# A second split in five products for two of layer 0's aggregates, with their left sums made one item per opportunity

## The chip, the cores and the metric

The kernel runs on one core of one Trainium2 chip. The metric is device time of one execution in microseconds (us), lower is better; where several executions were timed, the median is used. One execution was also taken by the hardware profiler, and all durations of single stages come from it.

## The reference

Two layers of a graph network on N = 2708 nodes with D = 1024 features, all fp32, `adj` an N×N matrix of 0 and 1:

```
# layer 0
h = relu(layernorm(x))
f = h @ Wf + bf;  g = h @ Wg + bg
e = relu(f @ g.T)                      # N x N
a = softmax(where(adj > 0, e, -9e15), axis=1)
x = x + a @ (h @ W + bW)
# layer 1
h = relu(layernorm(x)) @ W1
e = leaky_relu(h @ a1 + (h @ a2).T, 0.2)
a = softmax(where(adj > 0, e, -9e15), axis=1)
x = x + relu(a @ h)
```

The large parts are products of matrices: scores (N×D by D×N), the aggregate of the attention with the rows of h (N×N by N×D), and the projections (N×D by D×D). In layer 0 the kernel computes the aggregate of h first and multiplies it by W afterwards.

## The kernel before

**Tiling.** The N nodes for which attention is computed are split in NP = 5 panels of 576, 576, 532, 512 and 512 columns. Everything is kept transposed: an attention tile S holds 128 source nodes on its partitions and one panel's columns. The source nodes form NQ = 10 pairs of 128-row tiles and two left-over tiles (MONO and TINY); two pairs form a group, and there are NK = 5 groups. W = 512 is half of D, WH = 256 a quarter.

**Products.** Each big product is a 2×2 Strassen–Winograd product: seven products named M1, M5, M2, M6, M3, M7, M4 of half-size operands in place of eight. Their left operands are sums of rows of h, made once and kept in DRAM: `hg_d` for layer 0, `hr_d` for layer 1. Their right operands are sums of halves of attention tiles. A panel's halves are 288, 288, 266, 256 and 256 columns wide.

**Stages.** For each panel of layer 0 the program runs: scores (line 1425), then the left side of the next panel's scores (`project_q`), then the aggregate (`aggregate`, whose matmuls are at line 679 in `accumulate`), then the projection by W (`project`, line 1314). Panel 3's projection comes after panel 4's scores. Layer 1 has an aggregate and a projection per panel.

**The aggregate of layer 0.** `accumulate` runs one product after another. A product is 80 matmuls: 10 pairs × 2 tiles' halves, 4 column blocks `d`. The left operand is loaded by SP (line 139) as 512 KB tiles `hc`, one per product and group. Sums collect in PSUM banks gx (M1, M2), gy (M5, M3), gz (M6, M7), gv (M4), and gw for the left-over rows (`into_m15`, line 971). VectorE (its additions are all recorded at line 45) or ScalarE empties the banks; the results of each node column are multiplied by 1/sum at the end, in GpSimd for three of four blocks (`scale`, line 1021).

**The aggregate of layer 1.** Panels 1 to 4 of layer 1 use another function, `aggregate_quartered` (from line 1087). There every one of the seven products is split once more in seven: 20 matmuls of a quarter of the panel's columns each (`product`, line 1114), on banks gx, gy, gz and gu. The right sums ("quarter" tiles) come from `make`, 20 VectorE operations per product. The left sums are four more blocks in DRAM, `hs2_d`. They are prepared by work items that `put_quarters` creates, one per product and group: GpSimd reads the rows (`hq`, line 417), VectorE does four operations of 128x256, and GpSimd stores two blocks (line 143).

**Order of the work.** Work items stand in lists (`lazy`, `later`) and are run in program order at opportunities, the calls of `behind(rate)`: four per product of `accumulate` (after k = 2, 5 and 7 and at the product's end). Each call gives credit of `rate` (3.0 in layer 0), and an item costs what `put` was given, 1.7 for an item of `put_quarters`. `ahead[0]` items have their reads issued ahead of the one that runs. Each engine keeps the program's order; a tile framework assigns buffers and sets waits. The pools concerned are 54 `slot` buffers, 12 `stream` buffers of 4 KB per partition, and 8 PSUM banks.

The call around the change is in the main loop over panels:

```
spare[0], from_slots[0] = p > 0, p == NP - 1
G[p] = aggregate(0, p, S, got["sm"], then)
```

Of the kernel before, what the change touches and what calls it, by code (L numbers as in the profile page):

```python
# [57 lines left out]
def kernel(  # L58
# [95 lines left out]
    groups = [[q, q + 1] for q in range(0, NQ, 2)]  # L154
    group_of = {q: (i, j) for i, g in enumerate(groups) for j, q in enumerate(g)}
    assert sorted(group_of) == list(range(NQ))
    hg_d = [dram.tile([P, 7, len(g), W], FP, name=f"hg_d{i}") for i, g in enumerate(groups)]
    NK = NQ // 2
    WH = W // 2
    hr_d = dram.tile([P, 7, 2, 2, NK, WH], FP, name="hr_d")  # L160
    hs2_d = dram.tile([P, 7, 4, NK, WH], FP, name="hs2_d")
# [206 lines left out]
    def rows_h(q, ha, hb):  # L368

        i, j = group_of[q]  # L370
        for m, h in ((M1, ha[0]), (M5, ha[1]), (M2, hb[0]), (M4, hb[1])):
            store(hg_d[i][:, m, j], h)
# [3 lines left out]
    def sums_h():  # L376

        def fetch(q, two):
            i, j = group_of[q]
            for m in (M1, M2):  # L380
                two.append(stream("hr", (P, 2, W)))
                (load if "m" in got else by_scalar)(two[-1], hg_d[i][:, m:m + 2, j])
# [6 lines left out]
        def second(q, two):  # L389
# [3 lines left out]
            i, j = group_of[q]  # L393
            store(hg_d[i][:, M6:M7 + 1, j], two[0])
            store(hg_d[i][:, M3, j], b0)
            store(hg_d[i][:, M5, j], b1)
# [6 lines left out]
    BY_QUARTERS = (M1, M5, M2, M6, M7, M3, M4)  # L403
    made_quarters = {}

    def put_quarters(m, k, to=lazy):
# [3 lines left out]
        def fetch():  # L410
            if from_slots[0]:
# [7 lines left out]
        def go():  # L419
# [5 lines left out]
            for h in range(2):  # L425
                store(hs2_d[:, m, 2 * h:2 * h + 2, k], two[h])
            made_quarters[m] = made_quarters.get(m, 0) + 1
        put(1.7, go, fetch, to=to)

    def quarters_until(m):  # L430
        while made_quarters.get(m, 0) < NK:
            one(lazy if lazy else later)
# [491 lines left out]
    def aggregate(l, p, S, sm, then={}, rate=3.0):  # L924
# [29 lines left out]
        steps = [(m, i) for m in order_of_products for i in range(len(groups))]  # L954

        def left(m, q, d):
            i, j = group_of[q]
            at = steps.index((m, i))
            for m_, i_ in steps[at:at + (3 if l else 1)]:
                if (m_, i_) not in hc:  # L960
                    hc[m_, i_] = stream("hc", (P, 4, WH) if l else (P, 2, W))
                    load(hc[m_, i_], hr_d[:, m_, :, :, i_].rearrange("p h f c -> p (h f) c") if l else hg_d[i_][:, m_])
# [71 lines left out]
    def quarters_of(p, S):  # L1034
# [50 lines left out]
        return {"make": make, "right": right, "first": first, "fifth": fifth, "second": second, "fourth": fourth}  # L1085

    def aggregate_quartered(p, S, sm, of_right, then={}, fine=1.2):
# [12 lines left out]
        def product(m, n, ps, start):  # L1100
            quarters_until(m)
            if (m, 0) not in lasts:
                for i, of in enumerate((hr_d[:, m, :, :, NK - 1].rearrange("p h f c -> p (h f) c"), hs2_d[:, m, :, NK - 1])):
                    lasts[m, i] = stream("hl2", (P, 4, WH))
                    load(lasts[m, i], of)
# [3 lines left out]
            load(t, hr_d[:, m, i // 2, i % 2, :NK - 1] if raw else hs2_d[:, m, i, :NK - 1])  # L1109
# [11 lines left out]
        def left_over(banks, e, s, fresh):  # L1121

            two = stream("hl", (P, W + 2 * P))
            load(two, hgl_d[1][:, e])
# [44 lines left out]
        def with_second():  # L1169
# [4 lines left out]
                       M7: lambda: make(M3), M3: lambda: make(M4)}  # L1174
        left_out = None
        for m in BY_QUARTERS:
            V = [quad(*direct[m])[:, 2 * r:2 * r + 2] for r in range(2)] if m in direct else [v[:, :, :h] for v in in_pairs("V")]
# [40 lines left out]
            if m == M5:  # L1218
                of_right["second"]()
            if m == M5:  # L1220
                inverse.append(inverse_sums(p, sm))
# [357 lines left out]
    def rows_done(t, xt):  # L1579
# [14 lines left out]
        if panel_of[t] == NP - 1:  # L1594
# [18 lines left out]
            else:  # L1613
# [16 lines left out]
                if q == NQ - 1:  # L1630
                    for m in BY_QUARTERS:
                        put_quarters(m, q // 2, later)
# [17 lines left out]
        elif whole:  # L1650
# [3 lines left out]
            if quads_met[q // 2] == 2:  # L1654
                put(0.0, lambda: [put_quarters(m, q // 2) for m in BY_QUARTERS])
# [12 lines left out]
    ORDERED = (NP - 1,)  # L1668

# [98 lines left out]
    for p in range(NP):  # L1768
# [21 lines left out]
        G[p] = aggregate(0, p, S, got["sm"], then)  # L1790
        spare[0] = False
        if p == 0:
            flush()
# [156 lines left out]
```

## Time and profile before

| what | value |
|---|---|
| median of 3 runs | 3051.23 us (3044.36 to 3053.49) |
| profiled execution | 3049.19 us, of which the profiler's span is 3047.3 |
| TensorE (PE) busy | 2993.9 us, 98% of the span |
| VectorE (DVE) busy | 2047.6 us, 67% |
| ScalarE (ACT), GpSimd (POOL) busy | 536.8 us, 496.9 us |
| TensorE clock granted | 0.997 of full speed |
| DMA | 766.78 MB, mean 252 GB/s |
| layer 0's aggregates of panels 1, 2, 3 | 148.2, 137.1 and 132.0 us |

PE is the matmul part of TensorE and PEld its weight loads, which overlap it. SP issues the loads, and its queue is that of line 139. A share of busy time is an average over all stages; a stage is read from a window of its own. Buffer numbers are left out of tile names, so `hs_d` also stands for `hs2_d`.

### The profile page before, as it was taken

The numbers are of one execution on the slowest core, as the hardware profiler recorded it, in microseconds if no ns is written. First come the engines' busy times: TensorE is split into PE (matmuls) and PEld (weight loads), VectorE is DVE, ScalarE is ACT, GpSimd is POOL, SyncE is SP. The second block draws the span as 40 slices with busy tenths as digits, with TensorE's granted clock in tenths as the row PEclk, the third lists the DMA queues.
The fourth block names the chain that finished last, engine by engine and source line by source line (L and its number), as shares of the span: only waits on it lengthen the run. The fifth ranks groups of instructions, "written<-read, shape, count | busy, mean of one in ns | idle before, by whom it ended". The sixth has DMA issues, their size and how long they took to land.

```text
span 3047.3 us, 41722 instructions
## 1 busy us (share of the span) xinstructions
PE 2993.9 (98%) x14642; PEld 2294.2 (75%) x14642; DVE 2047.6 (67%) x4667; ACT 536.8 (18%) x880; POOL 496.9 (16%) x770
## 2 busy tenths in 40 slices
PE   8998999999999999999999999999999999999999
PEld 4576777667877588885888886784767959879695
DVE  5776794585742686616965276867878768887863
ACT  4420020020200121101210111302232121212200
POOL 1421111210112110223111111131212010020201
PEclk9999999999999999999999999999999999999999
DMA  6989878887466786768957588679768768878887
GB/s 232 302 271 272 311 276 308 264 286 235 133 236 165 228 273 195 247 156 251 292 188 251 179 241 258 223 292 335 245 212 264 263 202 299 294 265 297 264 294 268
DMA packets 392704, 766.78 MB, mean 252 GB/s; under 512 B 65728, under 2 KB 206944, under 8 KB 392464
## 3 DMA queue, kind: packets, MB, share of 16 engines
q1 hardware_dynamic: 332336, 584.80, 59.6%
q0 software_dynamic: 54464, 164.78, 16.1%
q10 hardware_dynamic: 5696, 14.55, 1.4%
q8 instruction: 116, 1.90, 0.2%
q14 instruction: 92, 0.75, 0.1%
HBM read 630.04 MB, written 138.11 MB: 252 GB/s over the span
## 4 chain that ended last, share of the span: by engine, by line
PE 73%; DVE 11%; issue 8%; DMA 5%; POOL 1%; ACT 1%; SPq 1%; POOLq 0%; DVEq 0%; ACTq 0%
PE sz L1425 6%; PE gy L679 6%; PE gz L679 6%; PE gz L1114 5%; PE gx L679 5%; PE sx L1425 4%; PE pz L1314 4%; PE sy L1425 4%; PE px L1314 4%; PE py L1314 3%; PE gy L1114 3%; PE gx L1114 3%; PE gv L679 3%; PE M_ps L591 3%; PE qz L679 2%
## 5 line engine op out<-in xcount | busy, mean ns | idle before, releaser
L1425 PE MATMUL sz<-B,As 128*128 128x288 f32 (+2 forms) x1200 | 292.0, 392 | 6.0 <-DVE st L45 5.1
L1425 PEld LDWEIGHTS sz<-B,As 128*128 128x128 f32 x1200 | 227.2, 190 | 55.2 <-DVE st L45 8.4
L1425 PE MATMUL sx<-B,As 128*128 128x288 f32 (+2 forms) x800 | 200.8, 394 | 12.4 <-DMA As<-hs_d 10.4
L1425 PE MATMUL sy<-B,As 128*128 128x288 f32 (+2 forms) x800 | 199.0, 392 | 0.0
L1425 PEld LDWEIGHTS sx<-B,As 128*128 128x128 f32 x800 | 152.5, 191 | 45.8 <-DMA As<-hs_d 9.5
L679 PE MATMUL gz<-Sa,hc 128*128 128x288 f32 (+2 forms) x800 | 185.8, 392 | 0.0
L679 PEld LDWEIGHTS gz<-Sa,hc 128*128 128x128 f32 x800 | 151.5, 190 | 32.2 <-issue 2.2
L1425 PEld LDWEIGHTS sy<-B,As 128*128 128x128 f32 x800 | 151.7, 190 | 30.6 <-DVE st L45 0.3
L1114 PE MATMUL gz<-quarter,hc 128*128 128x128 f32 (+2 forms) x1344 | 168.8, 279 | 3.8 <-DVE gT L45 3.7
L1114 PEld LDWEIGHTS gz<-quarter,hc 128*128 128x128 f32 x1344 | 160.6, 191 | 5.1 <-DVE gT L45 4.6
L143 POOL DMA_DIRECT2D out_dram<-x_res x164 | 81.2, 502 | 469.1 <-DVE x_res L45 461.9
L1314 PE MATMUL py<-w,ps 128*128 128x512 f32 x320 | 142.0, 593 | 0.0
L1314 PE MATMUL pz<-w,ps 128*128 128x512 f32 x320 | 142.0, 594 | 0.0
L1314 PE MATMUL px<-w,gT 128*128 128x512 f32 x320 | 141.1, 593 | 0.0
L679 PE MATMUL gy<-T,hc 128*128 128x288 f32 (+2 forms) x480 | 114.9, 402 | 3.8 <-DMA hc<-hg_d 3.8
L1314 PEld LDWEIGHTS pz<-w,ps 128*128 128x128 f32 x320 | 60.2, 190 | 76.2 <-issue 72.2
L1314 PEld LDWEIGHTS py<-w,ps 128*128 128x128 f32 x320 | 60.5, 190 | 75.1 <-issue 72.7
L591 PE MATMUL M_ps<-wgT,wfT 128*128 128x512 f32 x256 | 112.7, 596 | 1.6 <-ACT hsT L45 1.6
L1314 PEld LDWEIGHTS px<-w,gT 128*128 128x128 f32 x320 | 60.1, 190 | 71.3 <-issue 67.8
L679 PEld LDWEIGHTS gy<-T,hc 128*128 128x128 f32 x480 | 93.1, 194 | 24.7 <-DMA hc<-hg_d 4.3
L143 POOL DMA_DIRECT2D mk_d<-mask x55 | 35.9, 654 | 456.4 <-DVE mask L45 439.4
L45 ACT ACTIVATE P<-P 128x576 f32<-128x576 f32 (+3 forms) x111 | 72.1, 650 | 207.3 <-DVE P L45 207.2
(391 smaller groups left out, 5819.6 us busy)
## 6 DMA issues: line engine op xcount, KB each, us to landing
hc<-hg_d SPq DMA_DIRECT2D x175, 512.0 KB
As<-hs_d SPq DMA_DIRECT2D x150, 512.0 KB
hc<-hr_d SPq DMA_DIRECT2D x119, 512.0 KB
hc<-hs_d SPq DMA_DIRECT2D x112, 512.0 KB
w<-wt_d SPq DMA_DIRECT2D x96, 512.0 KB
w<-in_L_gnn_W_dram SPq DMA_DIRECT2D x72, 512.0 KB
md<-md_d SPq DMA_DIRECT2D x56, 512.0 KB
adj_i<-in_adj_dram SPq DMA_DIRECT2D x200, 128.0 KB
```

The source lines that it names most:

```text
L45: i = f(*a, **k)
L143: nc.gpsimd.dma_start(a, b)
L591: nc.tensor.matmul(ps, wfT[a][c // NH][:, c % NH, :], wgT[b][c], start=(c == 0), stop=(c == NC - 1))
L679: nc.tensor.matmul(ps[d], left(m, k, d), right(m, k), start=(start and k == 0), stop=(k == K - 1), skip_group_check=True)
L1114: nc.tensor.matmul(ps[:, d], lhs[:, d * P:(d + 1) * P], inner_right(m, n, k), start=(start and k == 0 and d == 0), stop=(k == NK - 1), ski ...
L1314: nc.tensor.matmul(ps, left[i][m][:, k, :], w_[k], start=(start and k == 0), stop=(k == NH - 1), skip_group_check=True)
L1425: nc.tensor.matmul(ps[:n, :h], lefts[q][:, i % 2, c, :n], B[m][c // 2][:, c % 2, :h], start=(start and c == 0), stop=(c == NH - 1), skip_g ...
```

## The change

- `hg_d` was five tiles, one per group; it becomes one tile, indexed by group and pair.
- `hs2_d` becomes a pair, one tile per layer.
- `SPLIT_EARLY = (2, 3)`: in layer 0 the aggregates of panels 2 and 3 use `aggregate_quartered`, at a rate of 3.0 with 1.2 after each quarter product. In it, layer 0 keeps M1 and M5 as plain products through `accumulate`; M2, M6, M7, M3 and M4 are split in seven each. M1's banks are emptied by eight ScalarE copies, M5's by four VectorE additions; the products' 2×2 blocks V are collected in two `stream` tiles each; the factor 1/sum is applied by VectorE.
- `make(M2)`, the right sums of the first split product, is called in the middle of M5, and the sums of columns after it.
- `put_quarters` gets the layer as an argument. For layer 0 an item reads one 512 KB block of `hg_d` and has a cost of 3.0, one item per opportunity. The 25 items (five products, five groups) are put when panel 0's aggregate ends, ahead of the items of layer 1 that are left from before, so they run in panel 1's aggregate.

The diff, cut to its core:

```diff
-    hg_d = [dram.tile([P, 7, len(g), W], FP, name=f"hg_d{i}") for i, g in enumerate(groups)]
+    hg_d = dram.tile([P, 7, NK, 2, W], FP, name="hg_d")
-    hs2_d = dram.tile([P, 7, 4, NK, WH], FP, name="hs2_d")
+    hs2_d = [dram.tile([P, 7, 4, NK, WH], FP, name=f"hs2_d{l}") for l in range(2)]
...
-    BY_QUARTERS = (M1, M5, M2, M6, M7, M3, M4)
+    BY_QUARTERS = ((M2, M6, M7, M3, M4), (M1, M5, M2, M6, M7, M3, M4))
     made_quarters = {}
 
-    def put_quarters(m, k, to=lazy):
+    def put_quarters(l, m, k, to=lazy):
 
         two = []
 
         def fetch():
+            if l == 0:
+                t = stream("hq", (P, 2, 2, WH))
+                nc.gpsimd.dma_start(t.rearrange("p f h c -> p f (h c)"), hg_d[:, m, k])
+                two.extend(t[:, :, h] for h in range(2))
+                return
             if from_slots[0]:
                 two.extend(slot(f"hq{h}", (P, 2, WH)) for h in range(2))
             else:
...
             sub(a11, a22, a11)
             sub(a12, a12, a11)
             for h in range(2):
-                store(hs2_d[:, m, 2 * h:2 * h + 2, k], two[h])
-            made_quarters[m] = made_quarters.get(m, 0) + 1
-        put(1.7, go, fetch, to=to)
-
-    def quarters_until(m):
-        while made_quarters.get(m, 0) < NK:
+                store(hs2_d[l][:, m, 2 * h:2 * h + 2, k], two[h])
+            made_quarters[l, m] = made_quarters.get((l, m), 0) + 1
+        put(1.7 if l else 3.0, go, fetch, to=to)
+
+    def quarters_until(l, m):
+        while made_quarters.get((l, m), 0) < NK:
             one(lazy if lazy else later)
     u = consts.tile([P, NC], FP, name="u")
...
         def fourth():
             for q in range(NQ):
                 sub(t1(q), wb_(q)[:, lo], wa_(q)[:, lo])
-        return {"make": make, "right": right, "first": first, "fifth": fifth, "second": second, "fourth": fourth}
-
-    def aggregate_quartered(p, S, sm, of_right, then={}, fine=1.2):
+        return {"make": make, "right": right, "operand": operand, "first": first, "fifth": fifth, "second": second, "fourth": fourth}
+
+    def aggregate_quartered(l, p, S, sm, of_right, then={}, fine=1.2, rate=3.0):
...
         lasts = {}
         def product(m, n, ps, start):
-            quarters_until(m)
+            quarters_until(l, m)
             if (m, 0) not in lasts:
-                for i, of in enumerate((hr_d[:, m, :, :, NK - 1].rearrange("p h f c -> p (h f) c"), hs2_d[:, m, :, NK - 1])):
+                rows = hr_d[:, m, :, :, NK - 1] if l else hg_d[:, m, NK - 1].rearrange("p f (h c) -> p h f c", h=2)
+                for i, of in enumerate((rows, hs2_d[l][:, m, :, NK - 1])):
                     lasts[m, i] = stream("hl2", (P, 4, WH))
-                    load(lasts[m, i], of)
+                    if l or i:
+                        load(lasts[m, i], of if i else of.rearrange("p h f c -> p (h f) c"))
+                    else:
+                        for h_ in range(2):
+                            load(lasts[m, i][:, 2 * h_:2 * h_ + 2], of[:, h_])
             t = stream("hc2", (P, NK - 1, WH))
             raw = n in (M1, M2, M4)
             i = {M1: 0, M2: 1, M4: 3, M6: 0, M3: 1, M7: 2, M5: 3}[n]
-            load(t, hr_d[:, m, i // 2, i % 2, :NK - 1] if raw else hs2_d[:, m, i, :NK - 1])
+            load(t, hs2_d[l][:, m, i, :NK - 1] if not raw else hr_d[:, m, i // 2, i % 2, :NK - 1] if l else
+                 hg_d[:, m, :NK - 1, i % 2, i // 2 * WH:(i // 2 + 1) * WH])
             last = lasts[m, int(not raw)][:, i]
             for k in range(NK):
                 for d in range(2):
...
         def left_over(banks, e, s, fresh):
             two = stream("hl", (P, W + 2 * P))
-            load(two, hgl_d[1][:, e])
+            load(two, hgl_d[l][:, e])
             cols = lambda b: slice(s.start + b * hb, s.start + (b + 1) * hb)
             for (a, b), ps in banks.items():
                 for d in range(2):
...
         before_next = {M1: lambda: make(M5), M5: with_second, M2: lambda: (of_right["fourth"](), make(M6)), M6: lambda: make(M7),
                        M7: lambda: make(M3), M3: lambda: make(M4)}
+        def sums_of_columns():
+            of_right["second"]()
+            inverse.append(inverse_sums(p, sm))
+
+        def collected():
+            if l == 0:
+                return [stream("V", (P, 2, h)) for r in range(2)]
+            return [v[:, :, :h] for v in in_pairs("V")]
+
+        if l == 0:
+            hc = {}
+
+            def left(m, q, d):
+                i, j = q // 2, q % 2
+                if (m, i) not in hc:
+                    hc[m, i] = stream("hc", (P, 2, W))
+                    load(hc[m, i], hg_d[:, m, i])
+                return hc[m, i][:, j, d * P:(d + 1) * P]
+
+            def first_product(d, ps):
+                nc.scalar.copy(quad(0, lo)[:, d], ps)
+                nc.scalar.copy(quad(1, lo)[:, d], ps)
+            exps_until(NQ)
+            of_right["fifth"]()
+            accumulate(left, of_right["operand"], NQ, h, (M1, M5), then,
+                       {M1: first_product, M5: lambda d, ps: add(quad(0, hi)[:, d], ps, quad(0, lo)[:, d])}, "g",
+                       {M5: sums_of_columns}, rate=rate, by_k=True, more={(M5, NQ // 2): with_second})
+
         left_out = None
-        for m in BY_QUARTERS:
-            V = [quad(*direct[m])[:, 2 * r:2 * r + 2] for r in range(2)] if m in direct else [v[:, :, :h] for v in in_pairs("V")]
+        for m in BY_QUARTERS[l]:
+            V = [quad(*direct[m])[:, 2 * r:2 * r + 2] for r in range(2)] if m in direct else collected()
             c11, c12 = (V[0][:, :, b * hb:(b + 1) * hb] for b in range(2))
             c21, c22 = (V[1][:, :, b * hb:(b + 1) * hb] for b in range(2))
             X = bank2("gx")
...
                 into_place(m, V, 1)
                 scale(m, 1)
             if m == M5:
-                of_right["second"]()
-            if m == M5:
-                inverse.append(inverse_sums(p, sm))
+                sums_of_columns()
             if m in then:
                 then[m]()
         left_out()
...
         return list(full(p)) + ([MONO, TINY][p - 1:p] if p in (1, 2) else [])
     ORDERED = (NP - 1,)
+    SPLIT_EARLY = (2, 3)
     def by_gpsimd(o, i, **k):
         tc.keep_in_program_order(nc.gpsimd.dma_start(o, i, **k))
...
             then[M6] = lambda: first_masks(NP - 1, 1)
             then[M7] = lambda: first_masks(NP - 1, 2)
         spare[0], from_slots[0] = p > 0, p == NP - 1
-        G[p] = aggregate(0, p, S, got["sm"], then)
+        if p in SPLIT_EARLY:
+            G[p] = aggregate_quartered(0, p, S, got["sm"], quarters_of(p, S), then)
+        else:
+            G[p] = aggregate(0, p, S, got["sm"], then)
         spare[0] = False
         if p == 0:
+            for m in BY_QUARTERS[0]:
+                for k in range(NK):
+                    put_quarters(0, m, k)
             flush()
             ahead[0] = 2
             for s in range(1, NP):
...
             then = dict(zip((M2, M6) if p else (M3, (M7, "middle")), (lambda p=p: take_shifts(p + 1), lambda p=p: take_weights(p + 1))))
         spare[0] = p < 2
         ahead[0] = 2 if p else 4
-        g = aggregate_quartered(p, S, sm, next_right, then, fine=1.0) if p else aggregate(1, p, S, sm, then, rate=4.0)
+        g = aggregate_quartered(1, p, S, sm, next_right, then, fine=1.0) if p else aggregate(1, p, S, sm, then, rate=4.0)
         hooks = {}
         if p + 1 < NP:
             next_right = quarters_of(p + 1, got["P"][0])
```

## The prediction

> **What bounds the kernel now.** I read the page's engine totals and slices first, then the chain of waits, then a table of windows over the stages that the diff touches.
>
> ```profile
> PE 2993.9 (98%) x14642; PEld 2294.2 (75%) x14642; DVE 2047.6 (67%) x4667; ACT 536.8 (18%) x880; POOL 496.9 (16%) x770
> PE   8998999999999999999999999999999999999999
> PEclk9999999999999999999999999999999999999999
> ```
>
> TensorE works 98% of the span at full clock. The share is an average, so the windows decide. Their columns are the window, its length, each engine's busy time, clock, DMA share and GB/s; the rows are layer 0's aggregates of panels 1, 2 and 3, then two aggregates of layer 1 that are already split twice.
>
> ```profile
> core 0: us, PE busy (x) PEld busy (x) DVE busy (x) ACT busy (x) POOL busy (x), PEclk, DMA share, GB/s
> 838.80:987.00 148.20, 148.20 (x630) 114.24 (x629) 47.80 (x110) 6.05 (x13) 27.82 (x28) 1.00 0.67 200
> ...
> 1235.80:1372.90 137.10, 137.10 (x630) 114.21 (x629) 45.08 (x109) 4.66 (x11) 29.60 (x34) 1.00 0.69 208
> 1610.50:1742.50 132.00, 132.00 (x630) 114.16 (x629) 47.21 (x117) 11.14 (x16) 20.42 (x21) 1.00 0.72 223
> 2519.00:2645.60 126.60, 123.93 (x1118) 122.19 (x1118) 101.61 (x279) 23.08 (x43) 4.41 (x10) 1.00 0.85 294
> 2699.00:2823.40 124.40, 122.11 (x1121) 120.66 (x1120) 99.56 (x279) 22.89 (x43) 3.93 (x8) 1.00 0.88 301
> ```
>
> In the first three PE never pauses, while DVE is a third busy. PE time taken out of them is end time. The last two show what a second split turns a stage into: 1.8 times the instructions, DVE at 80%, DMA near 300 GB/s, and 2.3 to 2.7 us without PE. The chain gives the price of a product (start, us, engine, tile, line, count):
>
> ```profile
> 1235.86 17.93 PE gx L679 x80
> 1253.79 17.93 PE gy L679 x80
> ...
> 1610.55 17.27 PE gx L679 x80
> ...
> 2552.83 4.53 PE gz L1114 x40
> ...
> 2715.55 4.47 PE gz L1114 x40
> ```
>
> A plain product is 80 records of 266 or 256 columns. A quarter product is 20 records of 133 or 128 columns, so each pair of them gives 2.265 or 2.235 us.
>
> **What the skill says.** The Trainium skill, "TensorE: Matmul & The Clock Gate", Back-to-back issue gap, gives 134 cycles at 128 columns and 262 at 256: halving the columns keeps 51% of the time. The trace agrees: 4.47/40 = 111.7 ns against 17.27/80 = 215.9, or 52%. So small matmuls aren't punished here. "DMA: Bandwidth & Descriptors", Issuing engines are not separate DMA queues, says that transfers of all issuers share 16 engines. The trace has a stretch that shows the ceiling (857 to 876 us: share 1.01, 397 GB/s). Same page, Anatomy of one DMA: 2.0 us plus bytes/436e3, an estimate of 3.2 us for the new 512 KB read of GpSimd; the page's DMA issues show 4.3 us for 256 KB, so I take longer than that. "PSUM — Partial Sum Buffer", Engine vs sequencer instructions: "ScalarE/VectorE/GpSimdE queues are strict FIFO." The slower rival rests on it, and DVE's timeline follows its program order.
>
> **1. PE time removed.** M1 and M5 stay plain. M2, M6, M7, M3 and M4 become seven quarter products each.
> - Panel 2 before: 4×18.13 (with left-over rows interposed) + 17.93 = 90.45, and four left-over groups of 2.45 = 9.8: 100.25 us. After: 5×7×2.265 = 79.3, and four groups of 2.49 = 10.0: 89.3. Gain **11.0**.
> - Panel 3 before: 4×17.46 + 17.27 + 4×2.37 = 96.6. After: 5×7×2.235 = 78.2, and 4×2.46 = 9.8: 88.1. Gain **8.5**.
> - PE's instruction order is otherwise the same. Gross **−19.5 us**.
>
> **2. DVE in panels 2 and 3.** Added in each: right sums 100×0.207 (the same operation in layer 1), five products' evictions and placements at 0.35 to 0.7, and the scaling by 1/sum (about eight of 0.70) that GpSimd did in two operations. Less what goes: 45 becomes about 91 us of some 126, below the layer-1 stages' 80%. The narrow place is the end of M5, where the first quarter eviction must follow all right sums of M2:
>
> ```profile
> 1269.14 0.43 DVE L45 TENSOR_TENSOR m<-gy,m 128x266 f32<-128x266 f32 x1 [7.21 <-PE gy L679]
> ```
>
> DVE idled 7.21 us there. The new work ahead of it is 20×0.207 + 8×0.35 = 6.9 us, which fits; then come reciprocals 3.6 and about 20 sums 4.1. The first eviction of Z comes near 1280.7, and PE wants its result at about 1281.7. One microsecond is left: cost 0 to 3.
>
> **3. Buffers and loads in panels 2 and 3.** Before, one 512 KB load fed 16 records (3.6 us of PE); after, one feeds 16 to 20 narrow ones (1.8 to 2.3), plus V tiles from the same 12 stream buffers. From the changed program's buffer assignment I counted the PE work between the instruction that frees a buffer and the first use of its next load: in layer 1's split stages the smallest lead is 11.6 us and the median 17.6; in panel 2 they are 7.4 and 13.6; in panel 3 the smallest are 2.7, 4.4, 4.9, 4.9 and the median 11.1, since two adjacency tiles for panel 4's masks hold stream buffers between M6 and M7. The last quarter tile of M6 also waits for a slot of M2's (leads 3.9 and 3.4). The chain shows what a late load costs:
>
> ```profile
> 2604.31 4.01 DMA hc<-hs_d
> ```
>
> A load landing in 4 us covers leads of 7 but not of 3. Bounds: 0 each if loads land in 3, 8 to 10 together if they take 8 under this load. I take the layer-1 gaps as they are, **+2.5** in panel 2, and **+3.5** in panel 3.
>
> **4. Panel 1 pays for the left sums.** 25 new items (5 products × 5 pairs of pairs) run there, one per opportunity, the next one's read issued one item ahead: a 512 KB read, four DVE operations (0.34 each = 1.4), two 256 KB stores. Layer 1's seven items that ran first there come after them. Today's panel 1 shows the pitch of such operations (8.46/25), and GpSimd issuing stores at 0.7 each once DVE delivers:
>
> ```profile
> 849.71 8.46 DVE L45 TENSOR_TENSOR hq<-hq 128x256 f32<-128x256 f32 x25
> ...
> 851.09 3.55 POOL L143 DMA_DIRECT2D hs_d<-hq  x5 [10.52 <-DVE hq L45]
> ```
>
> PE executes none of this. DVE's 47.8 us take +34 of 148, POOL's 27.8 take 25×(0.7+1.43) = +53: nothing there is full. What counts is order. An item's DVE operations wait for its read, and behind them in DVE's order stand the evictions that free PE's banks. With two items in flight, one takes c = (L + 1.4 + 1.4 + 0.3)/2, L being the read's landing. L = 4.4 gives 3.8, L = 6.1 gives 4.6; I take **c = 4.2**. Counted from item 12 at about 884 us, the additions of gw's banks stand behind 29 items and GpSimd's 5.06 us scaling, and M4's third column needs them at 965.7: this permits c = 4.4. The fourth addition before gw at 954.1, behind 26.5 items, permits 4.8. Traffic at c = 4.2 is 1.05 MB/4.2 = 250 plus 135 for the left operands, 385 GB/s against the 397 seen: no reserve. Bounds: 0, and 1.7 us per 0.1 us above 4.4. I take **+1.5**.
>
> **Edits at nothing.** One hg_d tile for five: loads still follow the same stores, and panel 0's order is unchanged. M1's four more ScalarE copies at 0.4 hide in an engine 5% busy there. SP issues 58 fewer loads in all, in the same order outside the two stages. The seven displaced items go to later opportunities; panel 4's and layer 1's reads of them come hundreds of microseconds on. GpSimd's bias transfers of panel 1's projection, behind it at 962 to 984 today, would slip to 977–993, with a first use at about 994: if c rises, they are late next.
>
> **Sum.** −19.5 + 2.5 + 3.5 + 1.5 = −12.0. The profiled execution took 3049.2 (span 3047.3, 1.9 around it), so 3037.2; it lies 2.0 below the median of 3051.2, so against the median **3039**. A measurement of this kernel can tell about 0.3%, or 9 us.
>
> **Rivals.**
> - *Loads starve PE in panels 2 and 3 (same).* A 512 KB load takes 8 us and not 4 to 5 beside 300 GB/s and the stores; leads of 2.7 to 8.5 then cost 8 to 10 us more, and the result is 3047 to 3049. For it: leads shorter than layer 1's. Against it: the layer-1 stages hold 300 GB/s with 2.3 to 2.7 us lost.
> - *Panel 1's items hold back DVE (slower).* If reads take L = 7.5 to 8 with the stores of the item before, c exceeds 5.2, the point where 1.7 us per 0.1 eats 12 us and more. At c = 6 PE waits 27 us for evictions before gw and M4, and the result is about **3065**. For it: stretch 857 to 876 is saturated today, and there one read took 10.5 us to land. Against it: 876 to 964 moves only 154 GB/s.
> - *All of it is covered.* With no wait at all, −19.5: 3031.7.
> - That the change doesn't do what it says is excluded: the changed order of PE has the 490 quarter products.
>
> **How the numbers follow.** Forecast case 0.52 (own range 3031 to 3045), starved loads 0.20, items holding DVE 0.20, all covered 0.08. The line of 0.3% lies at 3042: the covered case and four fifths of the forecast case are below it, 0.08 + 0.42 = **0.50** faster. The last fifth and the starved case, less 0.03 in which both rivals act, give **0.27** same; 0.20 + 0.03 = **0.23** slower. The range 3030 to 3060 reaches from the covered case over the starved one to c = 5.7 (13 steps of 1.7 us are 22, less 13.5: 9 above the median).
>
> **What would show it.** Right: windows of panel 2's and 3's aggregates shorter by 8.5 and 5, PE idle 2 to 4 us in each; PE idle in panel 1 below 3; hq operations spaced by about 4.2 us. Wrong: PE idle before gw or M4 in panel 1 released by DVE m or gT, or PE idle released by DMA hc in M6 and M7 of panel 3; the M5 place wrong, if V<-gz is the releaser in panel 2 near 1281.

## The result, and the profile after

The change made the kernel **slower by 1.7%**: 3101.29 us, median of 4 runs (3098.40 to 3105.59), against 3050.55 before; ratio 1.0172, 95% interval 1.0157 to 1.0187. Predicted were 3039 and a range of 3030 to 3060. The profiled execution took 3102.07, its span is 3100.3.

The page of the changed kernel first: engine totals, and busy tenths and clock in 40 slices of 77.5 us.

```profile
PE 2985.7 (96%) x15370; PEld 2309.6 (74%) x15370; DVE 2160.7 (70%) x5025; ACT 543.2 (18%) x900; POOL 530.6 (17%) x841
PE   8998999999995899998999999999999999999999
PEclk9999999999997999999999999999999999999999
```

TensorE has 8 us less to do than before (2993.9) and a 5 and a low clock in the thirteenth slice, which begins at 930 us: in panel 1's aggregate, a stage in which the change alters no matmul. The windows of the three aggregates (panels 1, 2, 3) say the same:

```profile
core 0: us, PE busy (x) PEld busy (x) DVE busy (x) ACT busy (x) POOL busy (x), PEclk, DMA share, GB/s
837.60:1022.50 184.90, 150.49 (x630) 115.16 (x629) 87.27 (x206) 6.05 (x13) 73.45 (x98) 0.91 0.79 273
1283.10:1414.90 131.80, 128.78 (x994) 121.95 (x993) 82.28 (x241) 8.21 (x21) 17.23 (x25) 0.99 0.82 279
1667.90:1795.10 127.20, 124.86 (x993) 119.11 (x993) 83.23 (x246) 9.39 (x22) 13.34 (x19) 1.00 0.91 298
```

The two split stages became shorter, 137.0 to 131.8 and 132.0 to 127.2. Panel 1's grew from 148.1 to 184.9 with the same 630 matmuls. The waits of PE (what waited, for whom, total, times, longest) name the two large losses:

```profile
engine line waited for: us in total, times, longest us
PE sum_ps L903 <- DVE gT L45: 34.3, 1, 34.3
PE py L1346 <- DMA w<-wt_d: 22.8, 2, 13.4
...
PE gz L1120 <- DVE V L45: 3.0, 1, 3.0
```

**First loss.** `sum_ps` is a bank in which PE sums the columns of attention, and `gT<-gy` is the addition that empties the banks gy. The VectorE timeline of panel 1 (start, length, operation, and in brackets the idle time before it and what ended it), with some rows left out:

```profile
937.98 1.80 DVE L45 TENSOR_TENSOR hq<-hq 128x256 f32<-128x256 f32 x4 [6.28 <-DMA hq<-hg_d]
...
958.02 3.52 DVE L45 TENSOR_TENSOR hq<-hq 128x256 f32<-128x256 f32 x8 [6.75 <-DMA hq<-hg_d]
972.51 1.80 DVE L45 TENSOR_TENSOR hq<-hq 128x256 f32<-128x256 f32 x4 [10.97 <-DMA hq<-hr_d]
974.23 1.18 DVE L45 TENSOR_TENSOR gT<-gy,u 128x288 f32<-128x288 f32 x3
```

and PE's line of sum_ps, before and after:

```profile
941.36 1.13 PE L903 MATMUL sum_ps<-sm,ones 128*128 128x288 f32 x4
```

```profile
974.74 2.29 PE L903 MATMUL sum_ps<-sm,ones 128*128 128x288 f32 x4 [34.27 <-DVE gT L45]
```

The gy products ended at 940.5. From 940 to 975 VectorE was busy for 10.4 of 35 us, but gT<-gy stands behind 26 left-sum items in its order, layer 0's 25 and one of layer 1. Before an item, or before two that came together, VectorE sat idle for 4 to 7 us until a read had landed. TensorE wants one of gy's banks for sum_ps and stands for 34.27 us. Items 12 to 25 took from 889.4 to 961.5: **5.2 us an item**. The 26th, layer 1's, took until 974.3, 12.8 us by itself: GpSimd issued its reads at 965.75, behind the stores of the items before, and VectorE was idle for 10.97 us. So 21.0 us of the wait, from 940.5 on, are layer 0's items, and 12.8 are this one.

**Second loss.** SP's timeline at the end of panel 2's aggregate, before and after (x is the number of loads), and then PE's line of the first `py`, before and after. py is the third product of the projection, x_res the rows of x to which the projection's result is added:

```profile
1335.35 10.10 SPq L139 DMA_DIRECT2D w<-in_L_gnn_W_dram  x4
1345.54 26.18 SPq L139 DMA_DIRECT2D x_res<-in_x_dram  x48
1371.82 3.78 SPq L139 DMA_DIRECT2D adj_i<-in_adj_dram  x8
1375.70 0.87 SPq L139 DMA_DIRECT2D w<-wt_d  x2
```

```profile
1400.02 5.50 SPq L139 DMA_DIRECT2D w<-in_L_gnn_W_dram  x4
1405.57 28.27 SPq L139 DMA_DIRECT2D x_res<-in_x_dram  x48
1433.94 3.78 SPq L139 DMA_DIRECT2D adj_i<-in_adj_dram  x8
1437.82 0.98 SPq L139 DMA_DIRECT2D w<-wt_d  x2
```

```profile
1388.78 7.13 PE L1314 MATMUL py<-w,ps 128*128 128x512 f32 x16
```

```profile
1444.43 9.60 PE L1346 MATMUL py<-w,ps 128*128 128x512 f32 x16 [13.43 <-DMA w<-wt_d]
```

The projection began at 1372.7 before and at 1414.9 after. Before, SP had issued the aggregate's last loads 37 us ahead of that; the fine products take up their loads so late that SP now gets there 15 us ahead. The 48 short loads of x_res take SP 0.55 to 0.59 us each. Before, they lay under the aggregate. PE comes to py 16 us after the projection's start; W's rows for it (`w<-wt_d`), behind x_res on SP, were issued 3.0 us after that start before and 22.9 after, when PE already stands.

### The profile page after: what moved, and what is told of

Its sections match the earlier page's. It is cut to its first block, busy times and chain, and to the rows that moved or that the text cites. A ratio compares the mean times of both kernels' runs of the same rounds, so it can differ in the third digit from the quotient of the medians.

```text
span 3100.3 us, 43906 instructions
## 1 busy us (share of the span) xinstructions
PE 2985.7 (96%) x15370; PEld 2309.6 (74%) x15370; DVE 2160.7 (70%) x5025; ACT 543.2 (18%) x900; POOL 530.6 (17%) x841
## 4 chain that ended last, share of the span: by engine, by line
PE 58%; issue 13%; DVE 13%; DMA 10%; POOL 3%; SPq 1%; ACT 1%; POOLq 0%; DVEq 0%; ACTq 0%
PE gz L1120 7%; PE sz L1457 5%; PE gx L1120 4%; PE gy L1120 4%; PE pz L1346 4%; PE gy L679 3%; PE sy L1457 3%; PE py L1346 3%; PE sx L1457 3%; PE M_ps L591 3%; PE px L1346 3%; DVE P L45 2%; PE gx L679 2%; DMA hq<-hg_d 2%; PE qx L679 2%
## 5 line engine op out<-in xcount | busy, mean ns | idle before, releaser
L1120 PE MATMUL gz<-quarter,hc 128*128 128x128 f32 (+2 forms) x1824 | 228.8, 279 | 6.9 <-DVE gT L45 3.7
L1120 PEld LDWEIGHTS gz<-quarter,hc 128*128 128x128 f32 x1824 | 217.5, 191 | 8.8 <-DVE gT L45 4.6
L1457 PE MATMUL sx<-B,As 128*128 128x288 f32 (+2 forms) x800 | 201.4, 395 | 11.6 <-DMA As<-hs_d 10.4
L45 DVE TENSOR_TENSOR hq<-hq 128x256 f32<-128x256 f32 x212 | 85.3, 429 | 101.0 <-DMA hq<-hg_d 58.5
L143 POOL DMA_DIRECT2D mk_d<-mask x55 | 35.7, 650 | 548.6 <-DVE mask L45 538.1
L679 PE MATMUL gz<-Sa,hc 128*128 128x288 f32 (+1 forms) x480 | 115.0, 400 | 0.0
L679 PEld LDWEIGHTS gy<-T,hc 128*128 128x128 f32 x480 | 92.6, 193 | 24.7 <-DMA hc<-hg_d 4.5
```

The source lines that it names most:

```text
L45: i = f(*a, **k)
L143: nc.gpsimd.dma_start(a, b)
L679: nc.tensor.matmul(ps[d], left(m, k, d), right(m, k), start=(start and k == 0), stop=(k == K - 1), skip_group_check=True)
L1120: nc.tensor.matmul(ps[:, d], lhs[:, d * P:(d + 1) * P], inner_right(m, n, k), start=(start and k == 0 and d == 0), stop=(k == NK - 1), ski ...
L1457: nc.tensor.matmul(ps[:n, :h], lefts[q][:, i % 2, c, :n], B[m][c // 2][:, c % 2, :h], start=(start and c == 0), stop=(c == NH - 1), skip_g ...
```

## The experiments

All stage lengths are read in PE's timeline, from the first matmul of a stage to the first of the next (us). "agg" is an aggregate, "proj" a projection, "sc 2" the scores of panel 2; "late" is panel 4's projection and layer 1's first aggregate. Medians and ratios (95% interval) are against runs of the kernel before on the same chip; the medians of before lie between 3048.5 and 3051.7.

| kernel | agg 1 | proj 1 | sc 2 | agg 2 | proj 2 | agg 3 | late | median | ratio |
|---|---|---|---|---|---|---|---|---|---|
| before | 148.1 | 61.8 | 137.4 | 137.0 | 52.9 | 132.0 | 49 + 151 | 3050.6 | 1 |
| changed | 184.9 | 73.5 | 137.4 | 131.8 | 68.9 | 127.2 | | 3101.3 | 1.0172 (1.0157–1.0187) |
| e1 | 148.1 | 61.8 | 137.4 | 126.8 | 70.1 | 126.8 | | 3050.7 | 1.0008 (0.9998–1.0017) |
| e2 | 182.0 | 70.7 | 137.4 | 137.0 | 52.9 | 132.0 | | 3095.5 | 1.0150 (1.0135–1.0166) |
| e3 | 187.0 | 69.9 | 137.4 | 133.3 | 67.4 | 133.0 | | 3100.2 | 1.0167 (1.0152–1.0182) |
| e4 | 158.7 | 61.8 | 137.4 | 169.5 | 77.7 | 128.1 | | 3117.7 | 1.0219 (1.0202–1.0236) |
| e5 | 228.2 | 70.6 | 137.4 | 129.6 | 71.1 | 127.6 | | 3157.4 | 1.0348 (1.0332–1.0363) |
| e6 | 148.1 | 61.8 | 149.8 | 126.8 | 53.5 | 127.8 | | 3052.6 | 1.0010 (1.0000–1.0020) |
| e7 | 156.0 | 61.8 | 137.4 | 158.5 | 65.8 | 142.3 | 49 + 152 | 3097.9 | 1.0154 (1.0140–1.0168) |
| e8 | 186.6 | 61.8 | 137.4 | 126.8 | 69.7 | 127.2 | | 3093.8 | 1.0143 (1.0127–1.0159) |
| e9 | 158.7 | 65.6 | 137.4 | 137.0 | 52.9 | | | 3072.0 | 1.0065 (1.0043–1.0087) |
| e10 | 164.2 | 77.3 | 137.4 | 137.0 | 52.9 | | | 3079.5 | 1.0093 (1.0076–1.0110) |
| e11 | 182.0 | 69.8 | 137.4 | 137.0 | 52.9 | | | 3091.2 | 1.0130 (1.0115–1.0145) |
| e12 | 148.1 | 61.8 | 137.4 | 126.8 | 52.9 | 126.4 | | 3035.4 | 0.9951 (0.9936–0.9967) |
| e13 | 163.1 | 61.8 | 143.4 | 163.8 | 52.9 | 129.4 | 49 + 152 | 3093.9 | 1.0137 (1.0113–1.0161) |
| e14 | 150.1 | 61.8 | 142.5 | 163.4 | 52.9 | 126.8 | 49 + 152 | 3079.6 | 1.0093 (1.0068–1.0118) |
| e15 | 149.5 | 61.8 | 144.2 | 132.4 | 52.9 | 127.2 | 73 + 182 | 3101.2 | 1.0170 (1.0153–1.0186) |
| e16 | 149.9 | 63.0 | 148.3 | 126.8 | 52.9 | 127.7 | 73 + 183 | 3104.4 | 1.0182 (1.0161–1.0203) |
| e17 | 149.7 | 61.8 | 139.1 | 126.8 | 52.9 | 147.3 | 70 + 151 | 3083.9 | 1.0116 (1.0094–1.0139) |
| e18 | 150.0 | 61.8 | 147.7 | 147.5 | 53.5 | 126.2 | 49 + 151 | 3069.5 | 1.0067 (1.0049–1.0085) |

### The two halves apart: e1, e2

```diff
# e1
-            for m in BY_QUARTERS[0]:
-                for k in range(NK):
-                    put_quarters(0, m, k)
...
-            load(t, hs2_d[l][:, m, i, :NK - 1] if not raw else
+            load(t, hs2_d[l][:, m, i, :NK - 1] if l and not raw else
# e2
-    SPLIT_EARLY = (2, 3)
+    SPLIT_EARLY = ()
```

> Leaves out the 25 left-sum items of layer 0; the quarter products that need them load the plain rows of hg_d instead, in blocks of the same size, so the values of panels 2 and 3 are others. Theory (the items cost the time, through VectorE's order, in panel 1's aggregate and its projection; panel 2's projection is late for another reason, SP's order): panel 1's aggregate falls from 184.9 to 148 and its projection from 73.5 to 62, panel 2's projection stays at 69: 3101.3 - 36.8 - 11.7 = 3053. Rival (the split stages themselves, with their loads and buffers, are what costs, and panel 1 only shows it first): not below 3090.

> The 25 items run as in the changed kernel, but no aggregate of layer 0 is split. Theory (items cost by themselves): panel 1's aggregate 185 and its projection 73 as in the changed kernel, panel 2's projection 53 as before: 3050.6 + 36.8 + 11.7 = 3099. Rival (the split is needed for the loss): 3052 to 3060.

Both came out as the theory had it. PE's waits of e1 and then of e2:

```profile
PE py L1347 <- DMA w<-wt_d: 15.6, 1, 15.6
```

```profile
PE sum_ps L903 <- DVE gT L45: 31.1, 1, 31.1
```

Without items there is no wait in panel 1; with items alone the wait is there. The items cost 45.6 us (3095.5 against 3049.9) and the split with plain rows 0.8: together 46.4 of the 50.7 measured. And e1 shows the split's own account: 10.2 and 5.2 won in the aggregates, 17.2 lost in panel 2's projection.

### Panel 2's projection: e3, e6, e12

```diff
# e3
-        ws = {m: load_W(l, m) for m in order[:2]}
+        ws = {m: load_W(l, m) for m in order[:3 if l == 0 and p in (1, 2) else 2]}
# e6 (on e1)
-    ORDERED = (NP - 1,)
+    ORDERED = (2, NP - 1)
# e12 (on e6)
-            if p in ORDERED and q in (2, 6):
-                (copy_residual if q == 2 else bias_residual)(p)
+            if p in (1, NP - 1) and q in (2, 6):
+                (copy_residual if q == 2 else bias_residual)(2 if p == 1 else p)
```

> The changed kernel, with one edit: in the projections of panels 1 and 2 the rows of W for the third product are loaded ahead of the x_res loads instead of behind them on SP's queue. Theory (48 short x_res loads and 8 to 12 mask loads at some 0.5 us each stand ahead of W on SP): the waits of py for W, 9.3 and 13.4 us, go: 3101.3 - 22.8 = 3078.5; up to 8 us of it may come back if x_res is late next, so 3078 to 3087. Rival (the transfers are slow because the DMA engines are full, whatever the order): py's or px's waits stay in sum above 18, 3097 or more.

e3 was a miss in time: the wait of py went, though GpSimd's transfers were as before, and the next product's rows, still behind x_res, were late by 11.6 and 3.9 us (pz for W). Moving one load past a queue that is 28 us long passes the wait on.

> As the run without items, and panel 2's residual rows are put in order ahead by GpSimd during its scores (the path that panel 4 has already: ORDERED = (2, 4)), so that SP issues 8 loads of x_res for them in place of 32, and GpSimd no bias transfers at the projection. Theory (SP reaches W's loads late because 48 short loads stand ahead): the wait of py for W, 15.6 us, goes and panel 2's projection is 52 to 55: 3050.7 - 16 = 3035 (3033 to 3040). Rival (W is late by its own buffers or by full DMA engines, and only its place in the queue changes): the wait stays over 8 in sum, 3043 or more.

> As the run without items and with panel 2's residual rows ordered ahead, but GpSimd copies those rows and adds the bias during the scores of panel 1 and not of panel 2. Theory (the 12 us that scores of panel 2 lost in that run came from these transfers, at 0.97 of the DMA engines; the scores of panel 1 run at 0.56): all three stages stay short, 126.8, 53.5 and 127, the scores of panel 1 lose at most 4: 3050 - 10 - 5 + 2 = 3037 (3033 to 3042). Rival (the transfers cost their time wherever they stand): 3045 or more.

e6 missed: it took the projection to 53.5 and gave the gain back in the scores of panel 2 (149.8), where GpSimd's transfers that add the bias in DRAM kept the DMA engines at 0.98 while they moved 175 GB/s. In e12, which came out as expected, they stand a panel earlier and cost nothing that the stages show. It is faster than the kernel before, by 0.5%, and the only one of these kernels that is; but it leaves the left sums out, so it shows what the split is worth and is not a kernel to use. SP's timeline and the two split aggregates of e12:

```profile
1350.25 5.50 SPq L139 DMA_DIRECT2D w<-in_L_gnn_W_dram  x4
1355.80 4.95 SPq L139 DMA_DIRECT2D x_res<-x_d  x8
1361.12 7.99 SPq L139 DMA_DIRECT2D x_res<-in_x_dram  x16
```

```profile
1238.30:1365.10 126.80, 126.80 (x993) 120.18 (x992) 81.25 (x237) 8.19 (x21) 11.85 (x18) 1.00 0.86 291
1602.60:1729.10 126.50, 124.92 (x994) 119.17 (x993) 83.24 (x246) 9.39 (x22) 13.38 (x19) 1.00 0.94 299
```

24 loads of x_res in 13 us in place of 48 in 28, and a split aggregate in which PE doesn't pause. SP reaches W only 15 us before the projection here too (1350.25, start at 1365.1): what changed is the queue behind that point, and W's rows for py went out 8.0 us after the start. GpSimd's bias transfers at the projection fell from 16 to 8 as well, in e6 and e12 alike; these two runs don't tell the two apart, and e3 does so for py alone. The split is worth 15.8 us by the stages, 14.4 by the medians, where its loads have room and its left sums cost nothing.

### What sets an item's period: e5, e8 to e11

```diff
# e5: the four operations on GpSimd
+            on = nc.vector if l else nc.gpsimd
-            add(a22, a21, a22)
+            on.tensor_tensor(a22, a21, a22, OP.add)
...
# e8
-        ahead[0] = 1 if p == 0 else 2
+        ahead[0] = 1 if p == 0 else 4 if p == 1 else 2
# e9 (on e2)
-                store(hs2_d[l][:, m, 2 * h:2 * h + 2, k], two[h])
+                if l:
+                    store(hs2_d[l][:, m, 2 * h:2 * h + 2, k], two[h])
# e10 (on e2)
-                t = stream("hq", (P, 2, 2, WH))
-                nc.gpsimd.dma_start(t.rearrange("p f h c -> p f (h c)"), hg_d[:, m, k])
+                two.extend(slot(f"hq{h}", (P, 2, WH)) for h in range(2))
+                for h in range(2):
+                    nc.gpsimd.dma_start(two[h], hg_d[:, m, k, :, h * WH:(h + 1) * WH])
# e11 (on e2): hs2_d[0] is [P, 7, NK, 2, 2, WH]
+            if l == 0:
+                store(hs2_d[l][:, m, k], whole)
```

> The changed kernel, with the four operations of each of layer 0's 25 items done by GpSimd instead of VectorE: the same reads, stores and traffic, but nothing of them stands in VectorE's order. Theory (VectorE's order is what holds back the evictions): the wait of sum_ps for gT, 34.3 us, falls under 8; what may be late next is GpSimd's own scaling at the end of panel 1 and its bias transfers, so panel 1's aggregate 149 to 158 and its projection 62 to 72: 3101.3 - 30 to - 48, 3053 to 3071. Rival (the items' traffic keeps TensorE waiting whatever engine adds): panel 1's aggregate stays above 175, 3090 or more.

e5 was the worst of all, and a miss. It showed that one item is enough. VectorE's timeline there:

```profile
1020.19 1.81 DVE L45 TENSOR_TENSOR hq<-hq 128x256 f32<-128x256 f32 x4 [79.76 <-DMA hq<-hr_d]
```

One item of layer 1 was left ahead of gT<-gy in VectorE's order. Its read stood behind all of layer 0's items in GpSimd's queue, so VectorE stood for 79.76 us, and PE waited 41.2 us for gT. Loads of hc were late too, 24.7 us in sum in panel 1.

> The changed kernel with the items' reads issued three items ahead in panel 1 instead of one. Theory A (an item's period is its read's latency shared by the few in flight): the period falls from 5.5 to about 4, sum_ps waits 8 to 15 instead of 34, 3075 to 3085. Theory B (the DMA engines or the 12 stream buffers set the period): the wait stays at 30 or more, or turns into waits for hc, 3095 to 3110.

> As the run with the items and no split (3095.5; panel 1's aggregate 182), with the stores of layer 0's 25 items left out: their sums are made and go nowhere. Theory A (the items' period of 5.4 us comes from their stores: 1 KB pieces on the DMA engines, and a read that waits for the landing of an earlier item's stores, whose buffer it takes): period under 4, the wait of sum_ps, 31 us, falls under 8: 3053 to 3063. Theory B (the read's own landing, 5.6 us with VectorE's 1.8 behind it, sets the period): period 4.5 or more, the wait stays over 15: 3072 to 3095.

> As the run with the items and no split, but the items' rows are read into two slot buffers by two reads of 256 KB, and not into one of the 12 stream buffers that the left operands of TensorE use: same bytes, one DMA more an item. Theory A (a read waits for the landing of stores two or three items before, because the ring of 12 stream buffers comes round): the reads start earlier, the period falls under 4.5 and sum_ps waits under 15: 3060 to 3080. Theory B (DMA engines, or the one GpSimd queue in which a read stands behind the stores): no change or worse, 3090 to 3105.

> As the run with the items and no split, but each of layer 0's items stores its four sums with one DMA of 512 KB in pieces of 4 KB, and not two of 256 KB in pieces of 1 KB: same bytes, two DMAs an item and not three. Theory A (the pieces and the count of stores set the period): period 4.0 to 4.5, sum_ps waits 5 to 15: 3062 to 3078. Theory B (the read sets it): within 5 us of 3095.

The periods, from the start of VectorE's twelfth item to the end of its twenty-fifth: 5.1 us in e2, e8 and e11, 4.5 in e9, 4.3 in e10. In e8 28 items stood ahead of gT<-gy, three of them layer 1's, and sum_ps waited 35.7 us. So neither reading further ahead (e8) nor larger pieces and fewer stores (e11) shortens it. Without the stores (e9) the 26 items were done by 934.7 and sum_ps didn't wait; PE waited 9.2 us before gv instead. The wait fell as in its theory A; the time (3072.0) and the period are those of theory B.

e10 lies in the range of its theory A, but not by its mechanism:

```profile
952.55 1.18 DVE L45 TENSOR_TENSOR gT<-gy,u 128x288 f32<-128x288 f32 x3
```

Here 22 items stand ahead of gT<-gy and not 26: in the order of this program, this addition and an item of layer 1 come before the last four of layer 0. The work lists alone, in which layer 0's items stand first, don't fix the order on an engine. The 22nd item ended at 952.6, in e2 at 945.9, so the items were no sooner done; sum_ps waited 14.2 us and not 31.1 because fewer stood ahead. Panel 1's projection lost 15.5 us in e10, against 8.9 in e2.

What sets the period is shown only in part. In the changed kernel's trace one of the reads of items 12 to 25 waited for stores to land (4.1 us, issued at 910.27). The other 13 left GpSimd's queue without a pause behind a store of an earlier item, and nearly all of these stores had just waited for VectorE's sums. So a read starts when an earlier item's sums are done: the period is a round trip of read, sums and stores, and not a read's latency divided by two. How much of e9's gain comes from this order, how much from the landing of the stores (whose buffer a later read takes) and how much from traffic is not shown: 860 to 940 us of e2 has the DMA engines at 0.93 with 332 GB/s, e9 at 0.76 with 278.

### Pace and place of the items: e4, e7, e13 to e18

```diff
# e4: cost 5.0. e7: cost 6.0 and SPLIT_EARLY = (3,)
-        put(1.7 if l else 3.0, go, fetch, to=to)
+        put(1.7 if l else 5.0, go, fetch, to=to)
# e13 (with e12's order of x_res): cost EACH = 6.0; early[0] is true from panel 1's aggregate until panel 2's begins
-        while spare[0] and not later and lazy and credit[0] > 0:
+        while (spare[0] or early[0] and lazy and lazy[0][0] == EACH) and not later and lazy and credit[0] > 0:
# e14 is e13 with e10's slots. e15 (on e14); e16 is e15 at 4.5
-        spare[0], from_slots[0] = p > 0, p == NP - 1
+        spare[0], from_slots[0] = p in (1, NP - 1), p == NP - 1
# e17 (on e14); e18 is e17 at 5.0
-            behind(fine)
+            was, spare[0] = spare[0], spare[0] and l > 0
+            behind(fine)
+            spare[0] = was
```

> The changed kernel, with one number changed: a left-sum item costs 5.0 and not 3.0, so that three run in five opportunities, some 17 in panel 1's aggregate and 8 in panel 2's. Theory (too many items stand in VectorE's order ahead of the evictions that PE needs at 940 us): 15 to 16 items stand there instead of 26, which permits 7 us an item against 5.4 to 5.7 measured: panel 1's aggregate back to 148 to 152, its projection to 62 to 66, panel 2's aggregate 0 to 6 longer: 3101.3 - 36.8 - 9 + 3 = 3058 (3052 to 3066). Rival (an item costs PE its time wherever it runs, by traffic): two thirds of the loss stay in panel 1 and the rest goes to panel 2: above 3085.

> The changed kernel with only panel 3 split, and a left-sum item at a cost of 6.0 instead of 3.0, one in two opportunities: some 14 of the 25 in panel 1's aggregate and 11 in panel 2's, ahead of layer 1's. Theory (the number of items between two evictions decides): panel 1's aggregate 148 to 150, panel 2's 137 to 141 (layer 1's displaced items come at the end of it), projections as before, panel 3's 127: 3050 - 5 + 2 = 3047. Rival (any item of this kind in a busy stage costs its own period): 25 items cost 1.5 us each or more, above 3080.

Both missed. The slower pace freed panel 1 in part (158.7 and 156.0, projection 61.8; 148 to 152 and 148 to 150 expected): 16 and 14 items stood ahead of gT<-gy, and sum_ps waited 0.3 and 4.8 us. But I had not counted the items of layer 1, which had used the same opportunities and were pushed into panel 2. In e4 its aggregate is split: VectorE waits 1 to 8 us for most of their reads, among evictions that the fine products need every 2 us. In e7 it is plain and still took 158.5: sum_ps waited 17.5 us for gT there, the first loss over again.

> Nothing left out: the changed kernel with a left-sum item at a cost of 6.0, and allowed also in panel 1's projection, panel 2's scores and its left side, so that some 15 run in panel 1's aggregate and the other 10 up to panel 2's aggregate; panel 2's residual rows are ordered ahead during panel 1's scores. Theory (few items between two evictions, and W's loads not behind x_res's): panel 1's aggregate 156 as with 15 items before (+8), 2 to 8 more in its projection and the scores of panel 2, panel 2's aggregate 127 to 132, its projection 54, panel 3's 127: 3037 + 8 + 5 + 3 = 3053 (3044 to 3064). Rival (an item costs 1.5 us or more wherever it runs): 3075 or more.

> As the spread run, with the items' rows read into slot buffers instead of the ring of stream buffers. Theory (the ring's reuse set the period: 5.1 us fell to 4.5 with slots): panel 1's aggregate 149 to 153; but the projection of panel 1, whose x_res tiles are slots too, may wait for W as in the other slots run: 3042 to 3060. Rival (in scores slots are scarce): the scores of panel 2 lose 10 or more, over 3065.

Both missed. e13, with the items still in the ring of stream buffers, left 163.1 in panel 1 (sum_ps waited 13.2, behind 14 items). e14 brought it to 150.1, with 11 items ahead and no wait, and its projection at 61.8; panel 2's still took 163.4. There VectorE and PE read:

```profile
1336.96 1.80 DVE L45 TENSOR_TENSOR hq<-hq 128x256 f32<-128x256 f32 x4 [4.44 <-DMA hq<-hr_d]
```

```profile
1332.58 3.82 PE L1120 MATMUL gy<-Sa,hc 128*128 128x133 f32 x16 [5.60 <-DVE V L45]
```

> Nothing left out: as the spread run with slots, and layer 1's left-sum items kept out of the two split aggregates (extra items only in panels 1 and 4). Theory (in the spread run with slots panel 2's aggregate took 163 and not 127 because eleven of layer 1's items, whose reads land 5 us late each, stood in VectorE's order between the quarter products' evictions): panel 2's aggregate 127 to 132; panel 4 and layer 1's first aggregate, which now hold 33 of these items, lose 0 to 8: 3079.6 - 33 + 4 = 3050 (3043 to 3056). Rival (panel 2 is late for the split and the items' last sums): 3070 or more.

> As the run before it, at a cost of 4.5 an item: 18 to 20 of the 25 items in panel 1's aggregate, the rest in its projection and the first part of panel 2's scores, none left for panel 2's aggregate. Theory: panel 1's aggregate 150 to 156, scores of panel 2 138 to 141, panel 2's aggregate 127: 3045 (3038 to 3054). Rival (four more items in panel 1 are enough to hold the evictions again): panel 1's aggregate over 160, 3058 or more.

> Nothing left out: the spread run with slots (cost 6.0), in which no left-sum item runs between the quarter products of layer 0; layer 1's items run in the plain products M1 and M5 of panels 2 and 3 and in panel 4, so that panel 4 and layer 1 hold as many as before. Theory (an item costs where its VectorE operations stand between evictions that TensorE waits for, and nothing where they stand early in a plain product): panel 1's aggregate 150, its projection 62, scores of panel 2 143, panel 2's aggregate 127 to 134, its projection 53, panel 3's 127 to 130, the rest as before: 3050 + 2 + 5 - 6 - 4 = 3047 (3041 to 3056). Rival (these items cost wherever they are put, as in the last two runs): 3070 or more.

> As the run before it at a cost of 5.0 for layer 0's items, so that all 25 are done before panel 2's aggregate. Theory: panel 1's aggregate 150 to 152, scores of panel 2 143 to 147, panel 2's aggregate 127 to 132, the rest as in that run: 3046 (3040 to 3055). Rival: 3070 or more.

e15 to e18 moved layer 1's items about, and all four missed their ranges. Where they were kept out, panel 2's aggregate is 126.8 (e16, e17; 132.4 in e15), and the loss turns up where they went: 24 us in panel 4's projection and 31 in layer 1's first aggregate (e15), 20 in panel 3's aggregate and 21 in panel 4's projection (e17), 21 in panel 2's (e18, the best with nothing left out, 0.7% slower than before). No place was found that takes 25 more of them for nothing. That no such place exists is not shown.

## Why the prediction was wrong

- **Part 4, panel 1's items, is the step that failed.** It put +1.5 us where 36.8 were measured in the aggregate and 11.7 in the projection behind it; e1 and e2 attribute them to the items. Three terms in it were wrong. The period was put at 4.2 and was 5.2. Part of that is the read: 4.2 stands for one of 5.3 us, and the median of the 25 was 6.1. Part is the formula, which gives (6.1 + 3.1)/2 = 4.6 for it. The deadline was read off the wrong instruction. I took gw at 954.1, but the next to need a bank is sum_ps, which ran at 941.4 before. Behind 26 items, counted from item 12 at 884 as the prediction does, that permitted (941.4 − 884)/14 = 4.1 us: even the chosen 4.2 was over it, and item 12 came at 889.4. And the last of the 26, layer 1's, was counted like the others and took 12.8 us.
- **The slower rival had the mechanism**: VectorE's order holds back an eviction and a slow item makes PE wait, priced at 27 us for c = 6. It rested on the Trainium skill, "PSUM — Partial Sum Buffer", Engine vs sequencer instructions, which calls the queues of VectorE and GpSimd strict FIFO (first in, first out), and e5's 79.76 us agrees with that. Its point of decision, 5.2, came from the same wrong deadline; at 5.2 the wait was 34.3.
- **"Edits at nothing" held a second error.** SP's loads were counted (58 fewer) and not timed. SP reaches the next stage's loads 15 us and not 37 ahead of it, so that W's rows stand behind 28 us of x_res loads when PE needs them; panel 2's projection took +16.0. e3 shows SP's order as the cause for py, and the whole goes in e6 and e12, which also halved GpSimd's bias transfers there. The warning that panel 1's projection would be late next named GpSimd's bias transfers; what was late was W, on SP, by 9.3 us.
- **Part 1 held in panel 2 and not quite in panel 3.** With all else out of the way PE's busy time fell by 10.3 of 11.0 and 7.1 of 8.5 (e12).
- **Part 3 held in panel 3 alone.** There PE waited 2.3 us, all of it for hc, against 3.5 predicted. In panel 2 no load was late. Its 3.0 us of PE idle are the narrow place at M5's end (gz waits for V), which part 2 bounded at 0 to 3 and the sum left at nothing. That the 2.5 put down for loads lies close to it is luck.
- **The sum.** The stages named changed by −5.3 and −4.8 (against −8.5 and −5.0), +36.8, +11.7 and +16.0: 54.4, and the spans differ by 53.0. The count of 490 quarter products under the rivals is wrong: the two panels hold 70 (2 × 5 × 7). Nothing in the sum rests on it.
- **DMA's ceiling.** 397 GB/s as "no reserve" was too kind: with the items the engines stood at 0.93 with 332 GB/s (e2, 860 to 940 us).

## What to carry to other kernels

When work is added in the idle time of an in-order engine, ask what stands behind its wait and which instruction needs that first, and count every instruction between: an idle engine is not a free one. A stage that consumes its loads in smaller steps can also shorten the lead with which the load queue reaches the next stage, here from 37 to 15 us; sum the issue times of what stands ahead of the next stage's first operand. And preparation that a split needs has to be placed together with the preparation that already used those gaps.

## What the runs showed of the hardware

Behind several waits of this kernel TensorE was slow for a few microseconds. Windows of the changed kernel around the 3.0 us wait at 1332 and behind the 13.4 us wait at 1444, columns as above:

```profile
1331.00:1339.00 8.00, 6.87 (x45) 6.87 (x46) 1.85 (x7) 0.00 (x0) 0.00 (x0) 0.79 0.50 167
...
1444.00:1454.00 10.00, 9.57 (x20) 3.94 (x23) 1.39 (x2) 0.00 (x0) 2.81 (x6) 0.73 1.07 362
1454.00:1462.00 8.00, 8.00 (x50) 3.97 (x50) 4.61 (x9) 0.00 (x0) 0.00 (x0) 1.00 1.06 316
```

The granted clock was 0.79 and 0.73 there and 1.00 in the next window. The 16 matmuls of 512 columns that followed the longer wait took 9.60 us against 7.03 for 16 at full clock, so this wait cost 2.6 us on top of its 13.4, which a sum of waits leaves out. Not every wait does it: around the one of 2.1 us in panel 3's aggregate (1735 to 1743) the clock stayed at 1.00.

In e6, four transfers of 512 KB and one of 80 KB add a bias in DRAM. They were issued from 1124 to 1128. From 1127 to 1147 the DMA engines stood at 0.98 with only 175 GB/s moved, and PE waited 10.2 us for a load of its scores.
